# Layer 1's transposed input from block loads of h and x, with its norm applied behind the product

## The chip, the cores and the metric

The kernel runs on one NeuronCore of one Trainium2 chip, in one launch. The metric is device time in microseconds of that core, the median of several runs. Abbreviations are those of the profile: PE is TensorE's matmuls, PEld its weight loads, DVE is VectorE, ACT is ScalarE, POOL is GpSimd and SP the queue that issues the DMAs here.

## The reference, cut to what matters

There are B = 64 graphs of N = 256 nodes with D = 256 features, in float32. Layer 0 is a recurrence over the 256 nodes, batched over the graphs; its result is h. Then come three layers, each with a residual and a layer norm:

```
x = layernorm(x + gru(x, adj))                            # layer 0: h is gru's result
x = layernorm(x + relu(A_norm @ (x @ W1.T + b1)))         # layer 1, A_norm = D^-1/2 adj D^-1/2
x = layernorm(x + relu(softmax(mask(q k^T)) v Wo + bo))   # layer 2, one head
x = layernorm(x + multihead(x, adj > 0) Wo + bo)          # layer 3, 8 heads of 32
# layernorm(x) = (x - mean(x)) / sqrt(var(x) + 1e-5), over the features
```

## The kernel before, in words

`_recurrence` (L71 to L909) works through the 256 steps of layer 0 and writes h to the DRAM tile `Hd`, laid out node, graph, feature: for one graph, two neighbouring nodes lie B x D x 4 = 64 KB apart. It takes a little less than half of the time, and its code isn't touched.

`_layers` (L912 to L1288) then computes layers 1 to 3, one graph after another. A graph's activations are a tile of 128 partitions x 2 x 256: node c x 128 + p stands in partition p. The methods of `Graph` each issue a few instructions; nothing is reordered afterwards (`manual_schedule`, L980), so every engine executes its share in the order in which the methods are called. The string `ROUND` (L1260) writes that order out. In a round five graphs are in work at once, each at another depth: L (the newest: residual of layer 0, degrees, first norm), A (layer 1), B (layer 2), C (layer 3's scores), E (layer 3's end and store). Ahead of the steps of a round `load` (L1030) is called for the graph that becomes L in the next round. In a steady round there is one graph of each letter.

These steps and lines are the ones to know:

- `load` issues 11 DMAs on SP: `xin` (x), `ad` (adj), 8 for `az` (L1040), `y` (h, L1045). `az` holds adj in blocks, so that a DVE block transpose (32 x 32 blocks, `adT_v`, L1076) gives the whole transposed matrix: the loads put block (i, j) where block (j, i) belongs, in runs of 32 floats, 128 bytes.
- `residual_0` (L1049) adds `xin` to `y` on POOL.
- `norm_a` takes mean and variance on DVE (L949, L950), adds epsilon (L952, DVE) and raises to -1/2 (L953, POOL). `norm_b` makes `shift` = -mean x rstd (L959, DVE) and applies scale and shift on ACT (L961), in place in `y`.
- `xT(l)` transposes the normed `y` on PE with 4 transposes (L987) into a PSUM bank and copies it to SBUF on ACT (L1094). It is called for layers 1, 2 and 3.
- `t` is layer 1's product with W1 (L997) and the bias (L1099, DVE); `g` multiplies by the adjacency, applies relu on ACT (L1105) and adds to `y` on POOL (L1108). `degrees_a` (L1061 to L1067), `degrees_b` (L1071) and `adT_s` (ACT, L1086) make the scaled adjacency that `g` needs, for the next graph.
- `masks` (L1113, POOL), `qk2`, `v2`, `s2` (L1140, L1011), `exp2` (L1018), `w2`, `pT2` (L987, copy L1153) and `f2` (L1159, L1163) are layer 2.
- `bias_3` stores the normed `y` to `Yd` (L1176, SP) and adds layer 3's bias on POOL (L1177). `s3.0` and `s3.1` are layer 3's scores for four heads each (L1195, 32 rows), the mask added on DVE (L1204), exp on ACT (L1205), the sum of two halves on POOL (L1207). `o3` makes the denominators (L1221) of the first four heads, the heads (L1230), and the denominators of the last four. `d3` divides (L1244 to L1246, DVE), `f3` is the last product (L1253), `store` writes out (L1256, SP).

PSUM has four banks for the products and transposes (tag `mm`), used in turn, and four for scores. All DMAs of these layers go out on SP, in order, so what follows a DMA that waits for its data waits as well.

Of the kernel before, what the change touches and what calls it, by code (L numbers as in the profile page):

```python
# [9 lines left out]
F32 = mybir.dt.float32  # L10
BF16 = mybir.dt.bfloat16
AF = mybir.ActivationFunctionType
ALU = mybir.AluOpType
# [6 lines left out]
P = 128  # L20
# [891 lines left out]
def _layers(tc, ident, Hd, Yd, x, adj, weights, out):  # L912
# [8 lines left out]
    nc = tc.nc  # L921
    nat, W2, W3, b1_r, b2_r, b3_r, cols = weights
    B, N, D = x.shape
# [5 lines left out]
    with ExitStack() as ctx:  # L929
        const = ctx.enter_context(tc.tile_pool(name="l_const", bufs=1))  # L930
        W1T = const.tile([P, 2, D], F32, name="W1T")
# [7 lines left out]
        io = ctx.enter_context(tc.tile_pool(name="l_io", bufs=3))  # L939
# [4 lines left out]
        def norm_a(y, t):  # L944

            mv = small.tile([P, 2, 2], F32, tag="mv", name=f"mv_{t}")
            for c in range(2):
                st = small.tile([P, 6], F32, tag="st", name=f"st_{t}_{c}")
                nc.vector.bn_stats(st, y[:, c, :])  # L949
                nc.vector.bn_aggr(mv[:, c, :], st)  # L950
            rstd = small.tile([P, 2], F32, tag="rstd", name=f"rstd_{t}")
            nc.vector.tensor_scalar(rstd, mv[:, :, 1], EPS, None, ALU.add)  # L952
            nc.gpsimd.tensor_tensor(rstd, rstd, mhalf, ALU.pow)  # L953
            return mv, rstd

        def norm_b(y, mv, rstd, t):

            shift = small.tile([P, 2], F32, tag="shift", name=f"shift_{t}")
            nc.vector.scalar_tensor_tensor(shift, mv[:, :, 0], -1.0, rstd, ALU.mult, ALU.mult)  # L959
            for c in range(2):  # L960
                nc.scalar.activation(  # L961
                    y[:, c, :], y[:, c, :], AF.Identity, bias=shift[:, c:c + 1],
                    scale=rstd[:, c:c + 1],
                )

        def bank(name, shape=(P, 2, D)):
            return ps.tile(list(shape), F32, tag="mm", name=name, bufs=4)

        for c in range(2):
# [2 lines left out]
                nc.tensor.transpose(pt[:, k, :], nat[:, c, k * P:(k + 1) * P], ident)  # L972
            nc.vector.tensor_copy(W1T[:, :, c * P:(c + 1) * P], pt)

        nc.vector.tensor_copy(bv, cols[:, 4, :].unsqueeze(2).to_broadcast([P, 2, P]))
        pb = bank("bv3_ps", (P, D))
        for k in range(2):
# [4 lines left out]
        def flipped(src, t):  # L982

            pt = bank(f"tr_{t}")
            for a in range(2):
                for c in range(2):
                    nc.tensor.transpose(  # L987
                        pt[:, a, c * P:(c + 1) * P], src[:, c, a * P:(a + 1) * P], ident
                    )
            return pt  # L990

        def product(lhsT, rhs, t):

            pm = bank(f"mm_{t}")
            for c in range(2):
                for k in range(2):
                    nc.tensor.matmul(  # L997
                        pm[:, c, :], lhsT[:, k, c * P:(c + 1) * P], rhs[:, k, :],
                        start=(k == 0), stop=(k == 1),
                    )  # L1000
            return pm

        def new(tag, t, bufs=2, shape=(P, 2, D)):
            return work.tile(list(shape), F32, tag=tag, name=f"{tag}_{t}", bufs=bufs)

        def rows(b):
            return b.unsqueeze(1).to_broadcast([P, 2, D])
# [14 lines left out]
        class Graph:  # L1022
# [4 lines left out]
                self.p_of = {}  # L1027
                self.p_sum = {}

            def load(self):  # L1030
                b = self.b
                self.xin = io.tile([P, 2, D], F32, tag="xin", name=f"xin_{b}")
                nc.sync.dma_start(self.xin, x[b].rearrange("(c p) d -> p c d", p=P))
                self.ad = io.tile([P, 2, N], F32, tag="ad", name=f"ad_{b}", bufs=4)
                nc.sync.dma_start(self.ad, adj[b].rearrange("(c p) m -> p c m", p=P))
                self.az = io.tile([P, 2, 8, 32], F32, tag="az", name=f"az_{b}", bufs=3)
                for j in range(4):
                    for a in range(2):
                        at = a * P + j * 32
                        nc.sync.dma_start(  # L1040
                            self.az[j * 32:(j + 1) * 32, a],
                            adj[b, :, at:at + 32].rearrange("(i r) c -> r i c", r=32),
                        )
                self.y = io.tile([P, 2, D], F32, tag="y", name=f"y_{b}", bufs=7)
                nc.sync.dma_start(self.y, Hd[:, b, :].rearrange("(c p) d -> p c d", p=P))  # L1045


            def residual_0(self):
                nc.gpsimd.tensor_add(self.y, self.y, self.xin)  # L1049

            def norm_a(self, l):
                self.mv = norm_a(self.y, f"{l}_{self.b}")

            def norm_b(self, l):
                norm_b(self.y, *self.mv, f"{l}_{self.b}")
# [37 lines left out]
                self.xT_sb = new(f"xT{l}", self.b)  # L1093
                nc.scalar.copy(self.xT_sb, pt)  # L1094

            def t(self):
                pm = product(self.xT_sb, W1T, f"t_{self.b}")
                self.t_sb = new("t", self.b)
                nc.vector.tensor_add(self.t_sb, pm, rows(b1_r))  # L1099

            def g(self):
                pm = product(self.adT_sb, self.t_sb, f"g_{self.b}")
# [63 lines left out]
            def qk3(self, s):  # L1166
# [5 lines left out]
                    )  # L1172
                setattr(self, f"qk3{s}", m)

            def bias_3(self):
                nc.sync.dma_start(Yd[self.b], self.y)  # L1176
                nc.gpsimd.tensor_add(self.y, self.y, rows(b3_r))  # L1177

            def v3(self):
# [78 lines left out]


        ROUND = """  # L1260
            A.xT.1 B.xT.2 E.o3 E.d3.0 B.qk2.0 C.norm_b.2 E.d3.1
            A.t B.qk2.1 B.v2 L.residual_0 B.masks L.degrees_a
            L.adT_v E.f3 L.degrees_b C.xT.3 L.adT_s A.g C.bias_3 L.norm_a.0
            C.qk3.0 C.qk3.1 E.norm_a.3 A.norm_a.1 L.norm_b.0 B.s2 B.exp2
            C.s3.0 C.v3 B.w2
            B.pT2 E.norm_b.3 E.store A.norm_b.1 C.s3.1 B.f2
            B.norm_a.2
        """.split()
        graphs = [Graph(b) for b in range(B)]
        graphs[0].load()  # L1270
        for t in range(-1, B + 3):
            if 0 <= t + 2 < B:
                graphs[t + 2].load()
            for step in ROUND:
                who, name, *args = step.split(".")
                b = t - "LABCE".index(who) + 1
                if 0 <= b < B:
                    getattr(graphs[b], name)(*map(int, args))

# [143 lines left out]
def kernel(ctx: ExitStack, tc: tile.TileContext, ins, out):  # L1423
# [25 lines left out]
    )  # L1449
    Yd = dram.tile([B, P, 2, D], F32, name="Yd")  # L1450
    found = _layers(tc, ident, Hd, Yd, x, adj, weights, out)
    with tc.If(found > 0):
        _layer_3(tc, ident, Yd, adj, l3, out)
# [36 lines left out]
```

## Time and profile before

| what | us |
|---|---|
| median of 3 runs | 3351.88 (3350.82 to 3364.95) |
| profiled execution, its own time | 3353.51 |
| its span, first to last instruction | 3351.7 |
| first and last transpose `tr_x` of the layers begin at | 1488.3 and 3321.6 |
| busy over the whole span: PE | 3131.6 (93%) |
| DVE | 2554.5 (76%) |
| ACT | 1838.6 (55%) |
| POOL | 1845.0 (55%) |
| loads of one graph on SP: `xin`, `ad`, `az`, `y`, first load to next `xin` (at the start) | 1475.4 to 1480.9 |
| POOL's add of two 128 x 512 tiles, one instruction (L1049) | 1.27 |
| DVE block transpose of 128 x 512 (L1076) | 0.71 |
| ACT copy of a transposed tile (L1094) | 0.59 |

The shares are averages over the recurrence, which waits for its own chain, and the layers, which keep PE full. What the change is worth is read from the layers' rounds: which engine has no gap there, and what waits last. Times in a timeline are counted from the start of the span. Starts of neighbouring instructions on DVE, ACT and POOL lie a little closer than their durations, since the records overlap by some hundredths of a us.

### The profile page before, as it was taken

Reading aid. Unit: us, or ns where it says so; the run is one execution under the profiler, and the core shown is the slowest. Engines: PE = TensorE matmul, PEld = TensorE weight load, DVE = VectorE, ACT = ScalarE, POOL = GpSimd, SP = SyncE. Lnnn points to the kernel's source line nnn. Section 1 sums busy time; section 2 is a strip of 40 time slices with the busy share of each in tenths; the row PEclk is TensorE's granted clock in tenths of the full one; section 3 lists DMA queues with packets and bytes.
Section 4 is the critical chain, followed back from the end, with each engine's and each line's share of the span. In section 5 each row is a group of like instructions: output and inputs, shape, how many; then the busy total and the mean of one; then the engine's idle time right before and its main releaser. Section 6 shows DMA issues by size and latency. Waiting matters only on the chain.

```text
span 3351.7 us, 78940 instructions
## 1 busy us (share of the span) xinstructions
PE 3131.6 (93%) x28584; PEld 2311.5 (69%) x28584; DVE 2554.5 (76%) x7381; ACT 1838.6 (55%) x4754; POOL 1845.0 (55%) x2165
## 2 busy tenths in 40 slices
PE   5799998998879998969999999999999999999997
PEld 4566665555545555547888888888888888888885
DVE  3487777776667878856888888888888888888885
ACT  0155554544445544535666666666666666666664
POOL 2377777766667878833444444444444444444443
PEclk7899999999999999989999999999999999999999
DMA  9856685788877675241221211122222222222210
GB/s 292 247 161 156 168 194 152 179 198 207 204 181 178 163 174 152 65 105 47 56 57 54 57 56 54 54 55 58 57 58 58 58 57 58 57 58 58 58 33 20
DMA packets 528608, 364.62 MB, mean 109 GB/s; under 512 B 246620, under 2 KB 494568, under 8 KB 522984
## 3 DMA queue, kind: packets, MB, share of 16 engines
q1 hardware_dynamic: 510520, 342.63, 39.6%
q10 hardware_dynamic: 17696, 16.91, 1.5%
q8 instruction: 229, 3.75, 0.5%
q14 instruction: 163, 1.34, 0.1%
HBM read 240.78 MB, written 99.61 MB: 102 GB/s over the span
## 4 chain that ended last, share of the span: by engine, by line
PE 77%; DMA 8%; DVE 7%; issue 2%; SPq 2%; ACT 2%; POOL 1%; DVEq 0%; ACTq 0%; POOLq 0%
PE mm L997 14%; PE rc L605 6%; PE rc L597 4%; PE s L1195 4%; PE mm_2f L997 3%; PE mm_3v L997 3%; PE mm_3f L997 3%; PE mm_2v L997 3%; PE late L521 3%; PE mm_t L997 3%; PE mm_2s L997 3%; PE mm_g L997 3%; PE mm_2w L997 3%; PE o L1230 3%; DVE ACC L630 3%; PE o L1221 3%
## 5 line engine op out<-in xcount | busy, mean ns | idle before, releaser
L1207 POOL TENSOR_TENSOR p3s<-p 128x256 f32<-128x256 f32 x512 | 358.9, 733 | 364.7 <-ACT p L1205 364.6
L630 DVE SCALAR_TENSOR_TENSOR ACC<-keep,S,ACC 128x128 f32<-128x128 f32 x1712 | 479.1, 343 | 16.9 <-POOL ACC L876 11.2
L997 PE MATMUL mm<-xT,weights 128*128 128x256 f32 x2048 | 483.7, 384 | 2.7 <-ACT xT L1094 2.7
L997 PEld LDWEIGHTS mm<-xT,weights 128*128 128x128 f32 x2048 | 386.0, 191 | 79.9 <-issue 25.5
L1204 DVE TENSOR_TENSOR p<-s,neg 128x512 f32<-128x512 f32 x512 | 317.6, 682 | 118.2 <-PE s L1195 118.2
L667 POOL TENSOR_TENSOR ACC<-ACC,far 128x384 f32<-128x384 f32 (+1 forms) x313 | 372.1, 1189 | 24.5
L663 POOL TENSOR_TENSOR far<-hs,S 128x384 f32<-128x384 f32 (+1 forms) x313 | 304.7, 973 | 4.7
L1205 ACT ACTIVATE p<-p 128x512 f32<-128x512 f32 x512 | 292.4, 626 | 1.6 <-DVE p L1204 1.6
L961 ACT ACTIVATE y<-y,shift,rstd 128x256 f32<-128x256 f32 x512 | 272.9, 599 | 26.6 <-DVE shift L959 22.7
L597 PE MATMUL rc<-WxT,xqT 128*64 128x256 f32 x2048 | 274.8, 390 | 1.1 <-issue 1.1
L1119 ACT ACTIVATE qk<-mm,weights 128x256 f32<-128x256 f32 x256 | 107.5, 471 | 301.9 <-PE mm L997 301.9
L805 POOL TENSOR_TENSOR ready<-ACC,dinv 128x128 f32<-128x128 f32 x255 | 102.1, 400 | 304.7 <-DVE ACC L630 304.2
L1108 POOL TENSOR_TENSOR y<-y,g 128x512 f32<-128x512 f32 x64 | 81.0, 1266 | 301.8 <-issue 301.8
L1244 DVE RECIPROCAL rT<-o 128x256 f32<-128x256 f32 x128 | 223.7, 1748 | 0.3 <-PE o L1221 0.2
L949 DVE BATCH_NORM_STATS2 st<-y 128x6 f32<-128x256 f32 x512 | 209.6, 409 | 13.1 <-POOL y L1108 10.3
L521 PE MATMUL late<-Hw,An 64*32 64x256 f32 x3840 | 166.7, 400 | 42.1 <-DMA Hw<-hs 18.8
L605 PE MATMUL rc<-WhT,rT 128*64 128x128 f32 x2048 | 172.5, 290 | 35.6 <-DVE rT L828 33.2
L824 ACT ACTIVATE rs<-rc 128x128 f32<-128x128 f32 x256 | 71.1, 278 | 245.0 <-PE rc L605 245.0
L605 PEld LDWEIGHTS rc<-WhT,rT 128*64 128x64 f32 x2048 | 109.1, 138 | 133.2 <-DVE rT L828 110.8
L953 POOL TENSOR_TENSOR rstd<-rstd,mhalf 128x2 f32<-128x2 f32 x256 | 173.8, 697 | 47.9 <-DVE rstd L952 34.6
L1066 POOL TENSOR_TENSOR dis<-dis,mhalf 128x2 f32<-128x2 f32 x64 | 44.9, 702 | 273.2 <-DVE dis L1065 261.8
L605 PE MATMUL rc<-WhT,xpT 128*64 128x128 f32 x2048 | 169.4, 286 | 18.1 <-ACT xpT L614 18.1
(162 smaller groups left out, 7255.4 us busy)
## 6 DMA issues: line engine op xcount, KB each, us to landing
xX<-in_x_dram ACTq DMA_DIRECT2D x16, 1024.0 KB
Us<-xu SPq DMA_DIRECT2D x64, 256.0 KB
xq<-in_x_dram SPq DMA_DIRECT2D x64, 256.0 KB
ACC<-Us SPq DMA_DIRECT2D x32, 512.0 KB
Es<-eu SPq DMA_DIRECT2D x64, 256.0 KB
early_sb<-Es SPq DMA_DIRECT2D x32, 512.0 KB
xin<-in_x_dram SPq DMA_DIRECT2D x64, 256.0 KB
ad<-in_adj_dram SPq DMA_DIRECT2D x64, 256.0 KB
```

The source lines that it names most:

```text
L521: nc.tensor.matmul(pb[g][q * T:(q + 1) * T, e, :], An[rows, b].rearrange("p u s -> p (u s)"), Hw[rows, b, :], start=True, stop=True,)
L597: nc.tensor.matmul(G[o * B:(o + 1) * B], xqT[a, i // 2][:, i % 2, kc, h * B:(h + 1) * B], WxT[:, kc, o, gates], start=False, stop=False, s ...
L605: nc.tensor.matmul(G[o * B:(o + 1) * B], hT[:, kc * B:(kc + 1) * B], WhT[:, kc, o, g], start=False, stop=(kc == 1), skip_group_check=True,)
L630: nc.vector.scalar_tensor_tensor(acc[:, 0, :], keep[:, j % 2, :], s, acc[:, 0, :], ALU.mult, ALU.add)
L663: nc.gpsimd.tensor_mul(tmp[:, 0:count, :], hs.unsqueeze(1).to_broadcast(shape), s.unsqueeze(2).to_broadcast(shape),)
L667: nc.gpsimd.tensor_add(acc, acc, tmp[:, 0:count, :])
L961: nc.scalar.activation(y[:, c, :], y[:, c, :], AF.Identity, bias=shift[:, c:c + 1], scale=rstd[:, c:c + 1],)
L997: nc.tensor.matmul(pm[:, c, :], lhsT[:, k, c * P:(c + 1) * P], rhs[:, k, :], start=(k == 0), stop=(k == 1),)
L1204: nc.vector.tensor_add(p, s_ps[i], self.neg3)
L1205: nc.scalar.activation(p, p, AF.Exp, scale=ISQ)
L1207: nc.gpsimd.tensor_add(both, p[:, 0, :], p[:, 1, :])
L1244: nc.vector.reciprocal(rT, o_ps[:, 1, :])
```

## The change

Layer 1's transposed input is made without PE. Two further tiles of blocks, `hz` (h) and `xz` (x), are loaded in the way of `az`, 8 DMAs each, all on SP. POOL adds them, and one DVE block transpose gives the transposed residual sum, not yet normed. The norm is moved behind the product: with W1 replaced by W1 minus its mean over the input features (made once, at the start of the layers), the product of the un-normed sum is free of the mean, and the division by the standard deviation is a factor per node, applied when the bias is added. The norm of `y` itself stays, for the residual.

The loads are split: `load_a` is called ahead of a round as before, with `y` before `az`; `load_b` is a step inside a round, `N.load_b`, behind `C.keep_3`, which is the store to `Yd` taken out of `bias_3`. N is the graph that becomes L in the next round. In the order, `A.xT.1` goes, `L.turn_0` comes in front of `C.s3.1`, `A.norm_b.1` is called before it too, and `E.norm_b.3` with `E.store` comes behind `C.s3.1`.

```diff
+        mean = const.tile([P, P], F32, name="mean")
+        nc.gpsimd.memset(mean, 1.0 / D)
+        pb = bank("w1_mean", (P, D))
+        for k in range(2):
+            nc.tensor.matmul(pb, mean, W1T[:, k, :], start=(k == 0), stop=(k == 1))
+        for k in range(2):
+            nc.vector.tensor_sub(W1T[:, k, :], W1T[:, k, :], pb)
...
-            def load(self):
+            def load_a(self):
...
+                self.y = io.tile([P, 2, D], F32, tag="y", name=f"y_{b}", bufs=7)
+                nc.sync.dma_start(self.y, Hd[:, b, :].rearrange("(c p) d -> p c d", p=P))
+                self.az = self.load_blocks("az", adj[b])
+
+            def load_b(self):
+                self.hz = self.load_blocks("hz", Hd[:, self.b, :])
+                self.xz = self.load_blocks("xz", x[self.b])
+
+            def load_blocks(self, tag, of):
+                to = io.tile([P, 2, 8, 32], F32, tag=tag, name=f"{tag}_{self.b}", bufs=3)
                 for j in range(4):
                     for a in range(2):
                         at = a * P + j * 32
                         nc.sync.dma_start(
+                            to[j * 32:(j + 1) * 32, a],
+                            of[:, at:at + 32].rearrange("(i r) c -> r i c", r=32),
                         )
...
             def residual_0(self):
                 nc.gpsimd.tensor_add(self.y, self.y, self.xin)
+                nc.gpsimd.tensor_add(self.hz, self.hz, self.xz)
+
+            def turn_0(self):
+                self.xT0 = new("xT0", self.b)
+                nc.vector.transpose(
+                    self.xT0.rearrange("p a m -> p (a m)"),
+                    self.hz.rearrange("p a i c -> p (a i c)"),
+                )
...
-            def t(self):
-                pm = product(self.xT_sb, W1T, f"t_{self.b}")
+            def t_a(self):
+                self.t_ps = product(self.xT0, W1T, f"t_{self.b}")
+
+            def t_b(self):
                 self.t_sb = new("t", self.b)
-                nc.vector.tensor_add(self.t_sb, pm, rows(b1_r))
+                for c in range(2):
+                    nc.vector.scalar_tensor_tensor(
+                        self.t_sb[:, c, :], self.t_ps[:, c, :], self.rstd0[:, c:c + 1], b1_r,
+                        ALU.mult, ALU.add,
+                    )
...
-            A.xT.1 B.xT.2 E.o3 E.d3.0 B.qk2.0 C.norm_b.2 E.d3.1
-            A.t B.qk2.1 B.v2 L.residual_0 B.masks L.degrees_a
-            L.adT_v E.f3 L.degrees_b C.xT.3 L.adT_s A.g C.bias_3 L.norm_a.0
+            B.xT.2 E.o3 E.d3.0 B.qk2.0 C.norm_b.2 E.d3.1
+            A.t_a A.t_b B.qk2.1 B.v2 L.residual_0 B.masks L.degrees_a
+            L.adT_v E.f3 L.degrees_b C.xT.3 C.keep_3 N.load_b
+            L.adT_s A.g C.bias_3 L.norm_a.0
             C.qk3.0 C.qk3.1 E.norm_a.3 A.norm_a.1 L.norm_b.0 B.s2 B.exp2
             C.s3.0 C.v3 B.w2
-            B.pT2 E.norm_b.3 E.store A.norm_b.1 C.s3.1 B.f2
+            B.pT2 A.norm_b.1 L.turn_0 C.s3.1 E.norm_b.3 E.store B.f2
             B.norm_a.2
```

More of the change, by code (lines that the diff above doesn't have):

```diff
@@ L1035, in load @@
                 nc.sync.dma_start(self.ad, adj[b].rearrange("(c p) m -> p c m", p=P))
-                self.az = io.tile([P, 2, 8, 32], F32, tag="az", name=f"az_{b}", bufs=3)
+                self.y = io.tile([P, 2, D], F32, tag="y", name=f"y_{b}", bufs=7)
[6 more added lines that the diff above has]
+                to = io.tile([P, 2, 8, 32], F32, tag=tag, name=f"{tag}_{self.b}", bufs=3)
                 for j in range(4):
@@ L1040, in load @@
                         nc.sync.dma_start(
-                            self.az[j * 32:(j + 1) * 32, a],
-                            adj[b, :, at:at + 32].rearrange("(i r) c -> r i c", r=32),
-                        )
-                self.y = io.tile([P, 2, D], F32, tag="y", name=f"y_{b}", bufs=7)
-                nc.sync.dma_start(self.y, Hd[:, b, :].rearrange("(c p) d -> p c d", p=P))
+                            to[j * 32:(j + 1) * 32, a],
+                            of[:, at:at + 32].rearrange("(i r) c -> r i c", r=32),
+                        )
+                return to
             def residual_0(self):
                 nc.gpsimd.tensor_add(self.y, self.y, self.xin)
+                nc.gpsimd.tensor_add(self.hz, self.hz, self.xz)
[5 more added lines that the diff above has]
+                )
             def norm_a(self, l):
                 self.mv = norm_a(self.y, f"{l}_{self.b}")
+                if l == 0:
+                    self.rstd0 = self.mv[1]
             def norm_b(self, l):
@@ L1173, in qk3, with keep_3 @@
                 setattr(self, f"qk3{s}", m)
+            def keep_3(self):
+                nc.sync.dma_start(Yd[self.b], self.y)
             def bias_3(self):
-                nc.sync.dma_start(Yd[self.b], self.y)
                 nc.gpsimd.tensor_add(self.y, self.y, rows(b3_r))
@@ L1269, in _layers @@
         graphs = [Graph(b) for b in range(B)]
-        graphs[0].load()
+        graphs[0].load_a()
+        graphs[0].load_b()
         for t in range(-1, B + 3):
             if 0 <= t + 2 < B:
-                graphs[t + 2].load()
+                graphs[t + 2].load_a()
             for step in ROUND:
                 who, name, *args = step.split(".")
-                b = t - "LABCE".index(who) + 1
+                b = t - "NLABCE".index(who) + 2
                 if 0 <= b < B:
```

## Prediction

> **What bounds the kernel now.** I read the page's slices first (TensorE at 9 tenths from slice 18 on), then the busy times by stretch over the layers' steady part, then the chain of waits inside one round, then the waits, and last the timelines of DVE, ACT, POOL and SP for the round from 2033.4 to 2061.8. Busy times in one steady stretch; columns are length, PE, PEld, DVE, ACT, POOL, granted clock, DMA share, GB/s:
>
> ```profile
> 2060.00:2560.00 500.00, 499.93 (x3400) 403.44 (x3399) 413.07 (x1019) 322.49 (x704) 234.96 (x301) 1.00 0.21 58
> ```
>
> TensorE has no gap at full clock. DVE is busy 83%, or 23.4 of a round's 28.34 us (s3.1 to s3.1, 2033.44 to 2061.78). Time can only come from what TensorE does, as long as DVE follows. The chain in the round, start and length in us:
>
> ```profile
> 2033.00 0.44 PE tr_p L987 x4
> 2033.44 1.08 PE s L1195 x16
> 2034.52 1.92 PE mm_2f L997 x8
> 2036.44 0.87 PE tr_x L987 x8
> 2037.32 0.57 PE o L1221 x8
> 2037.88 1.73 PE o L1230 x32
> 2039.61 0.83 PE o L1221 x8
> ```
>
> `tr_x` x8 is A.xT.1 and B.xT.2; half of it, 0.44 us, goes. The second group of denominators takes 0.83 where the first, the same eight instructions, takes 0.57: 0.26 us of hidden wait. The waits from 1560 to 3230 name it (total us, times, longest):
>
> ```profile
> DVE sm L1140 <- PE mm_2s L997: 50.7, 59, 0.9
> ...
> PEld mm_2f L997 <- ACT pT L1153: 19.6, 59, 0.3
> PEld o L1221 <- POOL p3s L1207: 16.3, 58, 0.6
> ```
>
> So 0.28 us a round is POOL's sums of the second half's exponentials coming late. DVE's slack before layer 2's scores (`sm`) is 0.86. The third thing to see is a lock between DVE and POOL; two DVE lines and two POOL lines of the same round:
>
> ```profile
> 2042.58 0.23 DVE L959 SCALAR_TENSOR_TENSOR shift<-mv,rstd 128x2 f32<-128x2 f32 x1
> ...
> 2052.46 1.27 DVE L952 TENSOR_SCALAR rstd<-mv 128x2 f32<-128x2 f32 x1
> ```
>
> ```profile
> 2042.18 0.62 POOL L1113 TENSOR_SCALAR neg<-ad 128x512 f32<-128x512 f32 x1
> ...
> 2052.45 1.27 POOL L1108 TENSOR_TENSOR y<-y,g 128x512 f32<-128x512 f32 x1 [4.66 <-issue]
> ```
>
> L952 on 128x2 has a median of 169 ns; here it lasts exactly as long as POOL's add.
>
> **What the Trainium skill says.** SBUF — State Buffer, "Who interferes with whom": a DVE instruction with two SBUF inputs, or in a two-port mode, and a GpSimd instruction reading SBUF exclude each other for the whole instruction. The trace agrees (above; L959 ranges from 135 to 722 ns). VectorE: DVE Perf Modes, "Why PSUM operands drop a tier": an fp32 PSUM operand keeps an operation at one element a cycle. The nearest row agrees: L1159, a scalar_tensor_tensor on 128x256 from PSUM, takes 487 ns, two in 1.04. DMA: Bandwidth & Descriptors, "Issuing engines are not separate DMA queues": all queues share 16 engines, so the 16 new issues cost SP time and engine time; the DMA share of 0.21 leaves room.
>
> **The change, part by part.**
>
> *Transposes.* A.xT.1 goes: 4 transposes, 0.44 us of TensorE, and a 0.59 us copy on ACT. All 64 graphs lose it, 62 of them in rounds where TensorE is full: 62 x 0.44 = **-27.3 us**.
>
> *The order at s3.1.* ACT now does only A's norm (1.05 instead of 2.08, timeline 2034.21 to 2036.19) ahead of s3.1's exponentials, so they begin at 2035.25 instead of 2036.19, then at DVE's pace of 0.60. POOL's fourth sum ends near 2038.8 instead of 2039.76. The second denominators, 0.44 earlier, reach their last head at about 2039.4: the wait goes with its whole sum, **-16.3**. Late next is the copy of B.xT.2, which stands behind E.norm_b.3 on ACT: exponentials to 37.65, norm to 38.7, copy to 39.25; B.qk2.0 wants it at 39.6. It holds by 0.3.
>
> *turn_0* is a 0.71 us block transpose (row L1076) where DVE waits 1.76 for s3.1: cost nothing, cover 1.0 left.
>
> *DVE's lateness*, the disputed part. From s3.1's end (2034.53) TensorE reached s2's end at 2056.66; with 0.44 and 0.28 gone, at 55.94. DVE: four adds to 36.94; E's shift moved here has two SBUF inputs and meets POOL's sums (0.70 each): +0.5, between 0.15 and 0.6. f2, norm_a.2, d3.0 as before, so C's shift comes at 43.1. POOL begins its rstd at 40.7, then the y add and the new hz add, 1.27 each (row L1049): to 43.95. The shift waits for that, DVE goes on at 44.05 instead of 42.73: +1.3. t_b is two scalar_tensor_tensors, 1.04, for one add that took 0.60: +1.7. DVE's 0.73 wait for E.f3 vanishes, f3's add starts at 50.3 (was 49.31), degrees_b ends at 51.05. ACT: adT_s 0.91 to 52.05, g's relu 0.84 to 52.95. POOL: y+g to 54.35, bias to 55.6, L's rstd to 56.3. DVE: L's shift to 56.45, and only then s2's product. That is **0.5 late** against 55.94. Behind it stand row max, exp2, s3.0's exponentials and the copies v3, w2, pT2, back to back on ACT, and pT2 feeds f2 on TensorE with about 0.1 spare. A stall of s at f2 delays the next s2 equally, so the lateness settles at 0.5 - s and s = 0.5 - s - 0.1 = 0.2. Over 60 rounds: **+12**; bounds 0 (small waits fall well) and 0.45 (another 0.5 late): 0 to +27.
>
> *Loads.* Sixteen SP issues more, 0.49 each (8 in 3.92 at L1040): 7.9. load_b waits for C.keep_3, which waits for C.norm_b.2, about 2044.8; it ends at 52.7 and nothing stands behind it until E.store, now gated by E.norm_b.3 near 38.7 of the next round (66.4). SP stays idle 13 us. The blocks are wanted by L.residual_0 one round later, past 69. As for the engines: over az's stretch (2065.4 to 2070.2) the share is 0.61, so a set of blocks is at most 2.9 us of all 16 engines; two more sets lift 5.9 of 28 to at most 11.7. Hidden. What this trace lacks is 128-byte reads of h, whose rows lie 64 KB apart; below nothing is excluded since the loads are added, and I take az's price. POOL has 50% idle; the hz add costs only through the lock. `mean`, one product and two subtractions at the start lie beside the wait for the first loads: nothing, at most 1.
>
> *The start.* Here SP is the path:
>
> ```profile
> 1476.45 3.91 SPq L1040 DMA_DIRECT2D az<-in_adj_dram x8
> 1480.40 0.45 SPq L1045 DMA_DIRECT2D y<-Hd  x1
> 1480.90 0.47 SPq L1033 DMA_DIRECT2D xin<-in_x_dram  x1
> ```
>
> A graph's loads were 11 issues, 5.5 us; now 27, 13.3. Graph 0's hz lands at about 1491, its t 5 us later than 1490.5. y of graph 0 moves ahead of az and waits about 1 us for the last store of h, holding az too. Graph 1's blocks, issued to 1503.3, hold POOL's residual add, its dis, adT_s and so A.g's relu: B.xT.2 of the next round near 1513.5 instead of 1504.6. Graph 2's fit in. **+9**, between 5 and 15.
>
> Sum: -27.3 - 16.3 + 12 + 9 = -22.6. The profiled execution took 3353.5 (span 3351.7 and 1.8 around it), so 3330.9; it stands 1.6 above the median of 3351.9, so **3329**.
>
> **The rivals.** *TensorE alone sets the round*: DVE's lateness stays inside pT2's spare. For it: DVE idles 4.9 a round and gets about 1 more of work; against: the chain above uses all slack. -27.3 - 16.3 + 9 = -35, time 3317.
>
> *A wait takes the place of the one removed*: xT.2's copy behind E.norm_b.3, or 0.3 to 0.5 more lateness, eats most of what the order frees: s = 0.45 and the start at 12: -27.3 - 16.3 + 27 + 12 = -5, time 3347. For it: margins of 0.3 and 0.1.
>
> *Slower: DVE and POOL become the loop*, through the shifts held by POOL's doubled residual add. The place is C.norm_b.2's shift and everything to s2. Above 0.5% slower needs -34.6 + 60 s > 16.8, s above 0.86, a lateness of 1.8 instead of 0.5. That takes the hz add waiting for its 16 landings inside POOL's queue (with masks behind it, 0.62, also holding the shift) and f3's add late on top. At s = 1.1 the time is 3383. Against: each of these was under 0.2 for az (DVE waits 0.2 before L1076).
>
> *The loads are no cover*: the h blocks cost so much that they land after residual_0, which needs over 17 us of transfer, six times az's bound. Then a round follows DMA, and the time is over 3400. Little speaks for it.
>
> **How the numbers follow.** A measurement of this kernel can tell about 0.5%, 16.8 us: faster is below 3335.1, slower above 3368.6. Forecast (3318 to 3342) 0.45; TensorE alone 0.25; wait for wait 0.18; DVE and POOL loop 0.09; loads 0.03. Faster: 0.45 x 0.8 + 0.25 x 0.96 = 0.60; slower 0.12; the same 0.28. The range reaches from TensorE alone with a short start, 3312, to wait for wait with a longer one, 3355.
>
> **What would show it.** Right: `tr_x` x4 in the chain, a second L1221 group near 0.57, a round near 27.8, `sm L1140 <- PE` nearly gone, PEld waiting for pT 0.2 longer, L959 near 0.9 on average where it meets the hz add, the first f2 about 8 late. Wrong: waits of POOL `hz` for DMA in steady rounds (the loads), PE waiting for xT2's copy (order), or a round at or above 28.34 (loop); a round of 27.6 speaks for TensorE alone.

## The result, and the profile after

The changed kernel takes 3315.5 us (median of 4 runs, 3310.9 to 3320.2) against 3355.3 for the kernel before in the same comparison. The ratio is 0.9876, with a 95% interval from 0.9858 to 0.9895: 1.24% faster. The profiled execution took 3310.9 us (span 3309.1) against 3353.5.

It helps to take the layers alone. The recurrence's code is the same, yet in the profiled executions of all eight kernels of this study the layers' first instruction (POOL's memset, L933) stands between 1471.2 and 1483.0 us. From there to the matmul of `count`, which closes the last round, it is 1873.5 us before and 1831.3 after: -42.2. Below, this is called the layers' time.

Busy times in the same steady stretch, columns as before (length, PE, PEld, DVE, ACT, POOL, clock, DMA share, GB/s):

```profile
2060.00:2560.00 500.00, 500.00 (x3414) 405.82 (x3407) 447.07 (x1091) 329.97 (x705) 265.13 (x328) 1.00 0.34 79
```

DVE rose from 83% to 89% of a stretch in which more rounds pass, the DMA share from 0.21 to 0.34, POOL from 47% to 53%. TensorE is as full as it was. This row tells nothing of the gain; the chain of waits of one round does:

```profile
2054.14 1.08 PE s L1231 x16
2055.22 1.93 PE mm_2f L1005 x8
2057.14 0.44 PE tr_x L995 x4
2057.58 0.57 PE o L1257 x8
2058.14 1.73 PE o L1266 x32
2059.87 0.43 PE o L1257 x8
```

`tr_x` is down from eight instructions to four, 0.44 us instead of 0.87, and the second group of denominators from 0.83 to 0.43. Together 0.83 us of a round. Layer 2's `mm_2f` begins at 1807.61 and again 44 rounds later at 3017.99: 27.51 us a round, where it was 28.34. The waits from 1560 to 3190:

```profile
PEld mm_2f L1005 <- ACT pT L1187: 19.9, 60, 0.3
...
DVE sm L1174 <- PE mm_2s L1005: 11.2, 55, 0.8
...
PEld o L1257 <- POOL p3s L1243: 0.7, 4, 0.2
```

POOL's late sums are gone as a wait (16.3 before). DVE still waits for layer 2's scores, 0.2 us a round instead of 0.86, so it is not late there. The wait for pT is what it was. POOL's addition into `hz` is in no line of the waits. On DVE and POOL the lock shows as it was argued; first DVE's shift of C, then POOL's new addition:

```profile
2036.30 0.76 DVE L959 SCALAR_TENSOR_TENSOR shift<-mv,rstd 128x2 f32<-128x2 f32 x1
```

```profile
2035.77 1.27 POOL L1067 TENSOR_TENSOR hz<-hz,xz 128x512 f32<-128x512 f32 x1
```

The shift began inside the addition and ended with it, at 2037.06; in the kernel before it took 0.23. The blocks of h and x cost 3.92 and 3.90 us of SP's time behind the store to `Yd`, with 12.6 us of idle SP after them:

```profile
2038.60 0.39 SPq L1210 DMA_DIRECT2D Yd<-y  x1
2039.03 3.92 SPq L1058 DMA_DIRECT2D hz<-Hd  x8
2042.99 3.90 SPq L1058 DMA_DIRECT2D xz<-in_x_dram  x8
2059.45 0.40 SPq L1292 DMA_DIRECT2D out_dram<-y  x1
```

At the start, the first f2 stands 62.9 us behind the layers' first instruction instead of 53.5: +9.4. With 60 rounds of -0.83, or -49.8, that makes -40.4 of the -42.2; the rest lies in the first and last rounds, which are not full.

### The profile page after: what moved, and what is told of

Same layout as the page of the kernel before. It is cut to its first block, busy times and chain, and to the rows that moved or that the text cites. A ratio compares the mean times of both kernels' runs of the same rounds, so it can differ in the third digit from the quotient of the medians.

```text
span 3309.1 us, 80053 instructions
## 1 busy us (share of the span) xinstructions
PE 3078.2 (93%) x28332; PEld 2275.6 (69%) x28332; DVE 2627.0 (79%) x7511; ACT 1833.1 (55%) x4690; POOL 1922.6 (58%) x2230
## 4 chain that ended last, share of the span: by engine, by line
PE 80%; DMA 7%; DVE 7%; issue 2%; SPq 2%; ACT 1%; POOL 1%; ACTq 0%; DVEq 0%; POOLq 0%
PE mm L1005 14%; PE rc L605 7%; PE rc L597 5%; PE s L1231 4%; PE late L521 4%; PE mm_3v L1005 4%; PE mm_2f L1005 4%; PE mm_2v L1005 3%; PE mm_3f L1005 3%; PE mm_g L1005 3%; PE mm_2s L1005 3%; PE mm_2w L1005 3%; PE mm_t L1005 3%; PE o L1266 3%; DVE ACC L630 3%; PE z_ps L605 2%
## 5 line engine op out<-in xcount | busy, mean ns | idle before, releaser
L1005 PE MATMUL mm<-xT,weights 128*128 128x256 f32 x2048 | 483.8, 384 | 2.7 <-ACT xT L1121 2.7
L1005 PEld LDWEIGHTS mm<-xT,weights 128*128 128x128 f32 x2048 | 386.1, 191 | 80.2 <-ACT xT L1121 28.8
L1241 ACT ACTIVATE p<-p 128x512 f32<-128x512 f32 x512 | 307.0, 629 | 3.6 <-DVE p L1240 3.0
L521 PE MATMUL late<-Hw,An 64*32 64x256 f32 x3840 | 165.5, 399 | 37.8 <-DMA Hw<-hs 14.3
L597 PEld LDWEIGHTS rc<-WxT,xqT 128*64 128x64 f32 x2048 | 140.6, 140 | 54.9 <-ACT rc L861 10.7
```

The lines of the kernel that those rows point to most:

```text
L521: nc.tensor.matmul(pb[g][q * T:(q + 1) * T, e, :], An[rows, b].rearrange("p u s -> p (u s)"), Hw[rows, b, :], start=True, stop=True,)
L597: nc.tensor.matmul(G[o * B:(o + 1) * B], xqT[a, i // 2][:, i % 2, kc, h * B:(h + 1) * B], WxT[:, kc, o, gates], start=False, stop=False, s ...
L1005: nc.tensor.matmul(pm[:, c, :], lhsT[:, k, c * P:(c + 1) * P], rhs[:, k, :], start=(k == 0), stop=(k == 1),)
L1241: nc.scalar.activation(p, p, AF.Exp, scale=ISQ)
```

## The experiments

The theory after the result: the change has two gains, the transposes and the order at s3.1, and they are not two independent savings; the order removes a loop over ACT and POOL which otherwise ends the round. One rival is that each part is worth its own time. Another, from the prediction, is that DVE's lateness takes some of the gain. Six kernels tell these apart, and test the start and the place of the loads. All ratios are against the kernel before.

**The order alone**, in the kernel before, with its transposes and loads:

```diff
-            B.pT2 E.norm_b.3 E.store A.norm_b.1 C.s3.1 B.f2
+            B.pT2 A.norm_b.1 C.s3.1 E.norm_b.3 E.store B.f2
```

> The kernel before with only the order at s3.1 changed (A.norm_b.1, C.s3.1, then E.norm_b.3 and E.store); the transposes and the loads stay as they were. Theory (the order frees the second denominators from POOL's late sums): the group of denominators after the heads falls from 0.83 to 0.43 us, a round from 28.34 to 27.94, 59 x 0.40 = 24 us faster, ratio 0.993; the wait of PEld o for POOL p3s goes from 16.3 to under 2 us. Rival (the order alone gives nothing, it only makes room for what the transposes leave): within 0.1% of before, the wait stays.

Measured: 0.9922 (0.9902 to 0.9942), the layers' time 25.1 us less than before. The chain of waits in a round:

```profile
2031.59 0.87 PE tr_x L987 x8
2032.46 0.57 PE o L1221 x8
2033.03 1.73 PE o L1230 x32
2034.76 0.43 PE o L1221 x8
```

All eight transposes are there, the second denominators take 0.43, and from `mm_2f` at 1806.07 to 3007.52 there are 43 rounds of 27.94. So 0.40 us a round come from the order, with the same work on every engine. From here to the changed kernel a round loses another 0.43: with the new order TensorE's 0.44 count in full.

**The old order** in the changed kernel:

```diff
-            B.pT2 A.norm_b.1 L.turn_0 C.s3.1 E.norm_b.3 E.store B.f2
+            B.pT2 E.norm_b.3 E.store A.norm_b.1 L.turn_0 C.s3.1 B.f2
```

> The changed kernel with the old order at s3.1: B.pT2, E.norm_b.3, E.store, A.norm_b.1, L.turn_0, C.s3.1. Theory (POOL's sums, not TensorE, then end the denominators): the 0.44 us taken from TensorE come back as wait, PEld o for POOL p3s rises to 0.7 or more a round, a round stays at 28.3, and with the start 9 us later the time is about 9 us above before, ratio 1.003. Rival (each part is worth its own): 27.3 us less and 9 more, ratio 0.994, the wait as before at 0.28.

Measured: 1.0018 (1.0009 to 1.0027), the layers' time 10.7 us more than before. From `mm_2f` at 1800.38 to 3019.16 there are 43 rounds of 28.34, the round of the kernel before, although TensorE has 0.44 less to do in each. The wait between 1600 and 3190 and, from the chain, how the denominators of one round end (the last two of them wait for POOL):

```profile
PEld o L1257 <- POOL p3s L1243: 30.8, 56, 0.6
```

```profile
2031.70 0.76 POOL p3s L1243
2032.45 0.04 issue
2032.50 0.62 PE o L1257 x2
2033.12 1.93 PE mm L1005 x8
```

The chain goes back from there over POOL's sums, ACT's exponentials of s3.1, its four norm instructions, the copies pT, w and v, the exponentials of s3.0, exp2, and DVE's `sm`, to the end of layer 2's scores; from the denominators it goes on through TensorE's products to the next scores. C.xT.3 lies in that loop, but A.xT.1 does not: its place is between f2 and the denominators, ahead of the point where TensorE waits for that loop. So the transposes alone are worth nothing, and what is left is the start. The rival with 0.994 is out. It also tells what bounded the kernel before: this loop, with TensorE waiting 0.40 in it.

**A longer lock.** One more POOL addition into a tile that nobody reads:

```diff
                 nc.gpsimd.tensor_add(self.y, self.y, self.xin)
+                wide = work.tile([P, 2, 2 * D], F32, tag="wide_l", ...)
+                nc.gpsimd.tensor_add(wide, ...)      # y and xin, each read twice: 128 x 1024
                 nc.gpsimd.tensor_add(self.hz, self.hz, self.xz)
```

> The changed kernel with one more POOL addition of 128 x 1024 into a tile that nobody reads, between the additions of y and of hz, 2.5 us. C's shift on DVE has two SBUF inputs, is issued during it and is held 1.3 us longer than now. Prediction's law (a lateness of DVE at layer 2's scores falls half on TensorE): lateness -0.18 + 1.3 = 1.1, less a spare of 0.1, half of it, 0.5 us a round, 30 us slower than the changed kernel, ratio to before 0.997. Rival 1 (all of it): 1.0 a round, 60 us, ratio 1.005. Rival 2 (it disappears in other slack): ratio as the changed kernel, 0.988.

Measured: 0.9938 (0.9920 to 0.9957), the layers' time 22.4 us more than the changed kernel's. POOL's addition and DVE's shift of C:

```profile
2053.77 2.36 POOL L1068 TENSOR_TENSOR wide_l<-y,xin 128x1024 f32<-128x1024 f32 x1
```

```profile
2054.18 1.97 DVE L959 SCALAR_TENSOR_TENSOR shift<-mv,rstd 128x2 f32<-128x2 f32 x1
```

An instruction on 128 x 2 takes 1.97 us, until POOL is through: 1.21 more than in the changed kernel, and that in every round. The round is 27.88 on average (43 from 1823.33 to 3022.32), 0.37 more. But hardly a round is 27.88 long: they last 27.5 and 28.24 by turns. TensorE in a long one, from f2 to f2:

```profile
2018.09 1.99 PE L1005 MATMUL mm_2f<-w,pT 128*128 128x256 f32 x8
...
2030.18 2.19 PE L1005 MATMUL mm_3f<-weights,oT 128*128 128x256 f32 x8
...
2046.33 1.99 PE L1005 MATMUL mm_2f<-w,pT 128*128 128x256 f32 x8 [0.36 <-ACT pT L1192]
```

Here E.f3 takes 2.19, in a short round 1.89: it waits for d3's division on DVE (`PEld mm_3f L1005 <- DVE oT L1286: 12.2, 28, 0.5` in the waits). DVE then begins on layer 2's scores 0.5 behind their end, and f2 waits for pT. The two waits make 0.74. DVE's work of the next round starts from s3.1, which stands ahead of f2; so a stall at f2 gives DVE 0.74 more until its next results are wanted. The next round loses nothing, and the round after it is long again. So the lateness reaches TensorE, neither in full in every round (rival 1) nor not at all (rival 2). The mean is the half of the prediction's law. Of the 1.21, about 0.2 is lost on DVE's way to the scores, 0.2 was its wait there, and less than 0.1 is spare behind pT, near the 0.1 predicted; 0.74 is left, and half of it is 0.37. The expectation had 30 us.

**Masks first.** The hz addition goes behind POOL's masks, so that the shift meets the shorter one:

```diff
-            ... L.residual_0 B.masks L.degrees_a
+            ... L.residual_0 B.masks L.sum_0 L.degrees_a      # sum_0 is the hz addition
```

> The changed kernel with POOL's masks (0.62 us) put between the additions of y and of hz, so that C's shift meets masks instead of the hz addition and is held about 0.1 us instead of 0.7. Theory (TensorE alone sets the round): DVE's wait for layer 2's scores grows from 0.2 to 0.7 us a round, the time stays within 0.1% of the changed kernel, ratio to before 0.988. Rival (DVE's lateness still costs TensorE something): 5 to 12 us faster than the changed kernel, ratio 0.984 to 0.986.

Measured: 0.9869 (0.9849 to 0.9890); the layers' time is 1.6 us above the changed kernel's, the round 27.51. The shift took 0.22. DVE's wait for layer 2's scores between 1600 and 3190:

```profile
DVE sm L1176 <- PE mm_2s L1005: 40.7, 58, 0.9
```

That is 0.70 a round against 0.2. DVE gains half a microsecond a round and nothing comes of it: in the changed kernel DVE's lateness costs nothing. The rival's 5 to 12 us are excluded by the round.

**The first two graphs by TensorE.** They get layer 1's transposed input as in the kernel before; no blocks of h and x are loaded or added for them:

```diff
             def load_b(self):
+                if self.b < 2:
+                    return
...
+            def xT_first(self):
+                if self.b < 2:
+                    self.xT(1)
...
+            A.xT_first B.xT.2 E.o3 E.d3.0 ...                 # t_a takes xT_sb, t_b adds b1
```

> The changed kernel, but the first two graphs get layer 1's transposed input as before (TensorE transposes of the normed y, no blocks of h and x for them). Theory (the start's 9 us are SP's issues of blocks for graphs 0 and 1): layer 1's first product begins about 4 us earlier, the first f2 9 us earlier, less 2 x 0.44 for the transposes; 8 us faster than the changed kernel, ratio to before 0.985. Rival (the start is set by something else, such as h's last store or the first norm): under 3 us, ratio 0.987 to 0.988.

Measured: 0.9846 (0.9827 to 0.9865), median 3304.8 us; the layers' time is 1822.5, 8.7 less than the changed kernel's and 50.9 less than before. The first f2 stands 52.5 behind the layers' first instruction (62.9 changed, 53.5 before); the round is unchanged at 27.51. So the whole of the start's loss was the block loads of two graphs on SP and what waited for them. By the layers' time this version is ahead of both kernels; the intervals of its ratio and of the changed kernel's overlap a little. It is 1 us ahead of the kernel before at the start; that `y` goes out ahead of the `az` blocks may be the reason, which was not tested.

**The loads ahead of the round**, behind `load_a`:

```diff
-            L.adT_v E.f3 L.degrees_b C.xT.3 C.keep_3 N.load_b
+            L.adT_v E.f3 L.degrees_b C.xT.3 C.keep_3
...
                 graphs[t + 2].load_a()
+                graphs[t + 2].load_b()
```

> The changed kernel with the blocks of h and x loaded ahead of the round, right behind load_a, not behind C.keep_3. Theory: SP is in order, so keep_3 waits behind 27 issues; bias_3 changes y in place and so waits for keep_3's transfer to have read it; it stands on POOL ahead of L's rstd, and DVE's shift and layer 2's scores follow. keep_3 goes out near 46.9 instead of 38.6 in the round of the changed kernel, bias_3 starts about 3 us late, half of the lateness falls on TensorE: 1.5 us a round, 90 us slower than the changed kernel, ratio to before 1.015. Rival (the place of the loads is of no account, SP idles 12 us a round): ratio as the changed kernel, 0.988.

Measured: 1.0207 (1.0182 to 1.0231), the layers' time 102.9 us more than the changed kernel's. A steady round is 29.3 on average, between 28.3 and 30.4. SP's queue and POOL's timeline in one round, whose f2 began at 2032.41:

```profile
2036.43 0.40 SPq L1292 DMA_DIRECT2D out_dram<-y  x1
...
2038.56 4.92 SPq L1058 DMA_DIRECT2D az<-in_adj_dram  x8
2043.53 4.86 SPq L1058 DMA_DIRECT2D hz<-Hd  x8
2048.43 3.91 SPq L1058 DMA_DIRECT2D xz<-in_x_dram  x8
2052.45 0.38 SPq L1210 DMA_DIRECT2D Yd<-y  x1
```

```profile
2049.59 1.27 POOL L1142 TENSOR_TENSOR y<-y,g 128x512 f32<-128x512 f32 x1 [3.56 <-ACT g L1139]
2054.69 1.27 POOL L1213 TENSOR_TENSOR y<-y,weights 128x512 f32<-128x512 f32 x1 [3.83 <-DMA Yd<-y]
2055.91 2.01 POOL L953 TENSOR_TENSOR rstd<-rstd,mhalf 128x2 f32<-128x2 f32 x3
```

The bracket is the idle time ahead of an instruction and what ended it. The store to `Yd` goes out behind the sixteen block loads; layer 3's bias, which changes `y` in place, waits for the store to have read it, 3.83 us here, the longest of 54, and 2.45 on average. L's rstd, the shift and layer 2's scores follow.

The loss is not half of that wait. SP issues 29 DMAs one behind the other from the output store to the store to `Yd`, 16.0 us here. The output store waits for E.norm_b.3, which stands on ACT behind the copy pT and s3.1's exponentials, and it goes out 4.0 us after f2's start. So a loop closes: output store, loads, store to `Yd`, bias, layer 2's scores, exponentials, pT, E.norm_b.3, output store. Over 47 rounds SP's part is 14.9 us on average, and a round is that part and 14.3 to 15.1 us more: what lengthens SP's part lengthens the round in full. In the changed kernel the same part has 13 issues and takes 6.7. The expectation's 1.5 a round was near the 1.8 measured in steady rounds, but by a rule that is not at work here. SP idles in this kernel too, the loads are the same, and the share of the DMA engines is 0.32: it is their place in the order that makes the difference.

## Why the prediction was right, and where it was mis-sized

The side was right, and the time lies in the range, near its lower end: 3315.5 against 3329. The forecast named as likeliest, TensorE slowed a little by a late DVE, is not what happened; its first rival, TensorE alone with 3317, is, and a round of 27.51 is the sign that the prediction gave for it (27.6). As changes, the forecast was -22.6, the rival -34.6, and measured are -39.8 in the comparison and -42.2 in the layers' time. That 3317 comes so near to 3315.5 is partly luck: the order's gain was sized too small, and the kernel before stands 3.4 higher in this comparison than the median from which the prediction counted.

**Transposes.** 0.44 a round was right (0.43 between the order alone and the changed kernel). Where they were booked was not. The prediction added them to the order's gain as if each stood alone, because the busy row had TensorE without a gap. The old order in the changed kernel shows that alone they give 0. The sum holds only because both were done together.

**The order.** The wait was named rightly, and that it would go. Its size was a term of the sum that was too small: 16.3 us in all, from the waits, where the chain has 0.40 a round, or 24. The prediction compared the second denominators, 0.83, with the first, 0.57. The first group isn't a clean measure: before, the waits list 9.9 us over 59 times, 0.17 a time, as an issue gap of TensorE's at L1221. The free group takes 0.43.

**DVE's lateness.** This is the step that failed: 0.5 late and 0.2 a round, 12 us, where DVE is 0.2 early and the cost is 0 (masks first). The chain had the right links in the right order, and several sizes that were a little large. Counted from DVE's first addition of s3.1 (2034.53 before; 2027.72 after, which is a round of 27.51 ahead of 2055.23):

| DVE or POOL begins | before | predicted | measured |
|---|---|---|---|
| d3.1's reciprocal, behind C's shift | 8.20 | 9.52 | 9.26 |
| degrees, behind t_b | 11.39 | 13.1 | 12.64 |
| f3's addition | 14.78 | 15.8 | 15.21 |
| POOL's y + g | 17.92 | 18.55 | 17.76 |
| layer 2's `sm` | 22.13 | 21.92 | 21.29 |

C's shift was held to POOL's end and no 0.1 beyond it. t_b's two instructions fill 0.79 from start to the next start, where f2's, the nearest row, fill 1.04. f2's rows write back to PSUM and t_b's to SBUF; whether that is the reason was not tested, and one row of 487 ns can't show by itself that the operation runs at one element a cycle. ACT's adT_s and relu took 1.64 from start to end (2043.71 to 2045.35) where 1.9 was summed with the steps between them. By the table the lock gave 0.26 less than summed, t_b 0.20, the way to f3's addition 0.13 and ACT 0.20. So DVE was ready for the scores 0.8 sooner than summed; TensorE came to them 0.1 sooner than summed, which leaves the 0.7 between 0.5 late and 0.2 early.

**The law of one half** was used to size that cost. The prediction had the lateness settle at a value between; the longer lock shows that it doesn't. By the prediction's own rule a stall of s takes s from the next lateness, so a late round and one in time follow each other, 28.24 and 27.5, and only their mean has the half. The loads ahead are no second case of it: there the loop goes through SP, and its length is the round.

**Loads.** Hidden in steady rounds, as said: SP idle for 12.6 us after them (13 predicted), DMA share 0.34 where at most 0.41 was worked out. The prediction gave what SP's order costs elsewhere less thought than it deserved. It named that load_b stands behind keep_3, but not that the reverse would hold up bias_3.

**The start.** +9 predicted, +9.4 measured, by the links that were named.

The second rival, a new wait in place of the old, fails: DVE was early, and B.xT.2's copy ended at 2059.89, 0.4 ahead of B.qk2.0's start at 2060.30. The third, a slower loop over DVE and POOL, exists as a mechanism, as the longer lock shows, but by its own sum it wants a lateness of 1.8, and DVE was 0.2 early. The last, loads that have no cover, fails too: POOL's addition into `hz` does not wait for their landing in steady rounds.

## What to carry to other kernels

When TensorE looks full and one group of its instructions takes longer than it should, look for the loop that ends there before counting any saved instruction: work removed ahead of the point where TensorE waits for that loop is worth nothing until the loop is shortened. Reordering ACT so that what others wait for stands ahead of a norm that nobody waits for gave 0.4 us a round for no work at all. In a queue that issues in order, put bulk loads behind the store whose buffer is about to be overwritten, and at a pipeline's start use the form that needs fewest issues. When a late engine stalls another, look at single rounds before believing their mean.

## What the runs showed of the hardware that was not expected

TensorE's busy time, as the profile counts it, does not show its waits: with the old order in the changed kernel the weight loads wait 0.55 us a round for POOL (30.8 in 56), 0.44 us of work is gone, and yet PE is busy for 1586.2 of 1590 us. The chain of waits and the length of the round showed it.

A DVE instruction on 128 x 2 held by POOL runs as long as POOL does, 1.97 us for one of 0.15, and it is counted as busy: DVE's rise from 413 to 447 us in 500 is partly such holding. With masks first, DVE's share between 1600 and 3190 is 87% at the same length of round.

The same recurrence, instruction for instruction, varied by 12 us among the profiled executions (its end between 1471 and 1483 us). From a single execution of each kernel, a change of 10 us in the layers was readable only in the layers' own time and in the length of a round.
